# Expert rows scattered to their tokens' rows instead of gathered, and unread matmuls at the start

## The chip, the cores and the metric

The kernel runs on one core of a Trainium2 chip. A core has five engines that run side by side, each in its own order: PE (TensorE, matmuls and the weight loads before them), DVE (VectorE), ACT (ScalarE), POOL (GpSimd) and SP (SyncE, which here only issues DMAs). SP, ACT and POOL issue DMAs, which all run on the core's 16 DMA engines. Data lie in HBM (DRAM), in SBUF (128 partitions) or in PSUM (eight banks, written by PE). The metric is the device time of one launch in microseconds; lower is better.

## The reference, cut to what matters

`x` is 625 x 1024; there are 20000 edges, sorted by `dst`, each of one of two types.

```
edge_index = jnp.stack([src, dst])
x = x + gnn(layernorm(x), edge_index, edge_type_2, ...)
x = x + ffn(layernorm(x))

gnn(h):  n = t5_layer_norm(h)
         out = n @ W_root + bias
         for r in range(2):  out += segment_sum((n[src] @ W_rel[r]) * w_r, dst) / max(cnt_r, 1)
         return h + elu(out) @ wo

ffn(h):  shared = mean over 2 of (gelu(h @ sW1 + sb1) @ sW2 + sb2)
         gates  = h @ rW + rb;   top 2 of 8, softmax over the two
         moe    = sum over the two chosen experts e of  w_e * (gelu(h @ W1[e] + b1[e]) @ W2[e] + b2[e])
         return shared + moe
```

## The kernel before

`gnn_ffn_kernel` runs `sparse_kernel`, and `dense_kernel` only if a flag says that the inputs don't fit the sparse layout; with these inputs it is not run. The framework keeps each engine's instructions in the order of the program unless one isn't ready in its own planning, and it sets the waits. `tc.issue_after(ins)` puts what is issued inside it behind `ins` on the same engine.

**Front.** The edges are turned into counts per (dst, src) pair by matmuls of one-hot rows. `edge_columns` brings the edge lists into columns (four transposes, `p_edge`). `count_windows` walks over 160 chunks `c` in groups of up to four: DVE writes the one-hots `oh_s` (L845, L846) and `oh_k` (L849), PE multiplies them (L858) into PSUM. Between the chunks the list `after[c]` runs other work at fixed `c`: `stats(t)` (mean and variance of the token tile `t`, and a centred copy `h` on ACT, L758), `to_columns(t, ...)` (eight transposes into `p_t`, L786, evicted by ACT, L792, and DVE, L789, into `nT`), `scales` (square roots on ACT, L709), `project(i)` (p_pr, 8 blocks of K that each show as two matmuls, L879), later `aggregate` and so on. `stats(0)` comes before the loop, behind `edge_columns`. The list `evicted` holds the last ACT and DVE evictions of tile 0; three orders are hung on it: ACT's square roots for two tiles come after `evicted[0]`, `stats(t)` for t > 0 after `evicted[1]`, and the one-hots of c = 8 after `evicted[1]`. All inputs come over SP in the order edges, x tile 0, W_root, x tile 1, tiles 2 and 3, tile 4, W_rel, wo.

**Middle.** The node projections and aggregations give `xh`; its layernorm goes to DRAM as `h2d`, `xh` itself as `x1d` (POOL, L953 and L954). `gate`, `route` and `slots` choose the two experts of each token and give each of the 2 x 625 (token, choice) pairs a slot in one of NJ = 11 tiles of 128 slots. Four tiles (NM2, numbers 0 to 3) hold halves or quarters of several experts, seven (`whole`) one expert each. `slots` makes `tok` (which token each slot holds, by ten small matmuls `p_tok` of one-hots with the token numbers `tid`), `idx` (in which slot each token's pair lies) and the flag `over`. PE runs the shared experts' first layer meanwhile. `fetch` gathers each tile's token rows from `h2d` with an indirect DMA on POOL (L1287), `expert_in` and `expert_mid` make the hidden rows `hjT`.

**End.** For each tile in `ORDER`, PE multiplies `hjT` with the experts' second weights into `p_yj` (L1382); where a tile holds several experts, ACT has copied their weights to `w2m` (L1374). DVE or ACT copies the two halves to `y` (L1386, L1388), and SP stores `y` plainly to DRAM: the first NA = 5 tiles to `ya`, the other six to `yb` (L1390). Then 20 indirect DMAs on POOL gather the rows back in token order: ten from `ya` after the fifth tile, ten from `yb` after the last (L1363); each `g[d, a]` holds token tile `d`'s choice `a` and is filled by both, since rows out of bounds are left alone. `w2m`, `y` and `g` share a pool of 15 buffers of 512 KB. PE goes on with the shared experts' second layer, `p_o` (L1429, L1431), five token tiles in eleven pieces, and DVE adds `p_o` and the weighted `g` to `x1` in an order fixed by `added` (L1405): p_o of tile 0, g of tile 0, p_o of tile 1, g of tile 1, then all g of tiles 2 to 4, then the other p_o. `store` sends each tile's rows to the output, 112 rows from SP and 13 from ACT (L1413); the last tile goes out in three pieces. The weights `sw2` and the rows `x1` for this stage are loaded from POOL before it (L1351, L1354).

Of the kernel before, what the change touches and what calls it, by code (L numbers as in the profile page):

```python
# [8 lines left out]
F32 = mybir.dt.float32  # L9
F16 = mybir.dt.float16  # L10
# [7 lines left out]
N = 625  # L18
D = 1024
# [24 lines left out]
NH2 = 3  # L44
NM2 = NH2 + 1
NQ = NJ - NM2
NA = NM2 + 1
HS = 64
QS = 32
NM = 5  # L50
# [402 lines left out]
def sparse_kernel(  # L453
# [34 lines left out]
    h2d = dram.tile([N, D], F32, name="h2d")  # L488
    x1d = dram.tile([N, D], F32, name="x1d")

    ya = dram.tile([NA * 128, D], F32, name="ya")
    yb = dram.tile([(NJ - NA) * 128, D], F32, name="yb")

    def ps_acc(name):
        return psum.tile([128, 512], F32, tag="acc", name=name, bufs=5)
# [74 lines left out]
    for m in range(NT):  # L570
# [7 lines left out]
    it = const.tile([TP, 128], F16, name="it")  # L578
    nc.gpsimd.iota(it, pattern=[[1, 128]], base=0, channel_multiplier=0,
                   allow_small_or_imprecise_dtypes=True)  # L580
    tid = const.tile([TP, NT], F16, name="tid")
    nc.gpsimd.iota(tid, pattern=[[TP, NT]], base=0, channel_multiplier=1,
                   allow_small_or_imprecise_dtypes=True)

    nt = 2 * NH2 + NQ
# [116 lines left out]
    def rsqrt(v, eps, name, n=1):  # L702

        c = small.tile([TP, 4, NT], F32, tag="rsq", name=name)
        c = [c[:, i, :n] for i in range(4)]
        with ExitStack() as order:
            if n == 2:
                order.enter_context(tc.issue_after(evicted[0].ins))
            nc.scalar.activation(c[3], v, AF.Sqrt, bias=epsc[eps])  # L709
        nc.vector.reciprocal(c[0], c[3])  # L710
        nc.vector.scalar_tensor_tensor(c[1], v, eps, c[0], op0=ALU.add, op1=ALU.mult)
        nc.vector.scalar_tensor_tensor(c[2], c[1], -0.5, c[0], op0=ALU.mult, op1=ALU.mult)
        r = small.tile([TP, NT], F32, tag="rsqo", name=name + "o")[:, :n]
        nc.vector.scalar_tensor_tensor(r, c[2], 1.5, c[0], op0=ALU.add, op1=ALU.mult)
        return r
# [61 lines left out]
    evicted = []  # L777
    nT = fbig.tile([128, KD, N], F32, name="nT")

    def to_columns(t, row, colT, scaled):  # L780
# [41 lines left out]
    def count_windows(between):  # L822
        accs = {}
        for cs in groups:
# [141 lines left out]

    for t, (c0, c1) in enumerate(((0, 3), (4, 9), (13, 19), (16, 22), (20, 26))):
        if t:
            at(c0, stats, t)
        at(c1, to_columns, t, None, nT, True)  # L970
    at(30, transpose_vec)
    at(6, scales, 0, 2)
    at(18, scales, 2, 4)
# [127 lines left out]

    idx = const.tile([TP, 2, 2, NT], I32, name="idx")
    wab = const.tile([TP, 2, NT], F32, name="wab")
    tok = const.tile([128, NJ], I32, name="tok")
    ej = const.tile([1, nt + 4], I32, name="ej")

    def slots():
# [79 lines left out]
        nc.vector.tensor_scalar(full, full, 127, None, op0=ALU.bitwise_and)  # L1189

        pc = const.tile([TP, 2, 2, NT], F16, name="pc")
        nc.vector.tensor_copy(pc[:, 0], full)
# [4 lines left out]
        for a in range(2):  # L1197
            nc.vector.tensor_tensor(oh[:, a], it[:, None, :].to_broadcast([TP, NT, 128]),
                                    pc[:, 0, a][:, :, None].to_broadcast([TP, NT, 128]), op=ALU.is_equal)
            nc.vector.tensor_tensor(oj[:, a], it[:, None, :NJ].to_broadcast([TP, NT, NJ]),  # L1200
                                    pc[:, 1, a][:, :, None].to_broadcast([TP, NT, NJ]), op=ALU.is_equal)
            nc.vector.tensor_mul(oj[:, a], oj[:, a], tid[:, :, None].to_broadcast([TP, NT, NJ]))
# [25 lines left out]
        over = const.tile([1, 3], F32, name="over")  # L1228
        nc.vector.tensor_tensor(over[:, 0:1], end_w[:1, NE - 1 :], taken[:1, 0:1], op=ALU.add)
        nc.vector.tensor_scalar(over[:, 0:1], over[:, 0:1], NQ + NH2 + 0.5, None, op0=ALU.is_gt)  # L1230
        nc.vector.tensor_scalar(over[:, 1:2], end_h[:1, NE - 1 :], 2 * NH2 + 0.5, None, op0=ALU.is_gt)
        nc.vector.tensor_scalar(over[:, 2:3], end_q[:1, NE - 1 :], 4.5, None, op0=ALU.is_gt)
        nc.vector.tensor_reduce(flagf[:, 1:2], over, axis=AX.X, op=ALU.add)
        nc.vector.tensor_tensor(flag, flagf[:, 0:1], flagf[:, 1:2], op=ALU.add)
        return named

# [119 lines left out]
    gs = {}  # L1356

    def gather(part, src):
        for d in range(NT):
            for a in range(2):  # L1360
                if part == 0:
                    gs[d, a] = gat.tile([128, D], F32, tag="y", name=f"g_{d}_{a}")[:TP]
                nc.gpsimd.indirect_dma_start(  # L1363
                    out=gs[d, a], out_offset=None, in_=src,
                    in_offset=bass.IndirectOffsetOnAxis(ap=idx[:, part, a, d : d + 1], axis=0),
                    bounds_check=src.shape[0] - 1, oob_is_err=False)

    ORDER = (*whole[:1], *range(NM2), *whole[1:])
    w2m = {}
    for j in ORDER:  # L1370
        for a, _, e in parts(j)[1:]:
            for k in range(HK):
                w2m[j, a, k] = gat.tile([128, D], F32, tag="y", name=f"w2m_{j}_{a}_{k}")
                nc.scalar.copy(w2m[j, a, k][:, None, :], w2a[:, bass.ds(e, 1), k, :])  # L1374
    for n, j in enumerate(ORDER):
        y = gat.tile([128, D], F32, tag="y", name=f"ys_{j}")
        for s in range(2):
            at = slice(s * 512, (s + 1) * 512)
            p = ps_acc(f"p_yj_{j}_{s}")
            for k in range(HK):  # L1380
                for a, b, e in parts(j):
                    made = nc.tensor.matmul(p[a:b], hjT[:, j, k, a:b],  # L1382
                                     w2m[j, a, k][:, at] if a else w2a[:, bass.ds(e, 1), k, at],
                                     start=(k == 0), stop=(k == HK - 1))
            if s or n < NA - 1:
# [18 lines left out]

    def add_experts(d):
        for a in range(2):
            add(x1[:, d, :], gs[d, a], wab[:, a, d : d + 1], x1[:, d, :])

    def store(d, at):
        for g, eng in zip(PARTS, (nc.sync, nc.scalar)):
# [67 lines left out]
```

## Time and profile before

| What | us |
|---|---|
| Three timed runs, median (lowest to highest) | 316.52 (314.95 to 316.57) |
| The profiled execution: its own time | 315.64 |
| its span, first to last instruction | 313.8 |
| PE, first matmul of the counts | 9.56 |
| PE busy in the span | 294.8 (94%) |
| DVE busy in the span | 179.5 (57%) |
| ACT, POOL busy | 110.5, 65.3 |
| DMA issues, median to landing: `ya`, `yb` stores (512 KB) | 7.2, 5.6 |
| gathers `g` from `ya`, from `yb` | 6.7, 8.6 |
| gathers `xs` in the middle | 4.4 |

The span is the profiler's time from the first to the last instruction; the launch's own time has 1.8 us around it. A busy row of the profile has 40 digits, each the busy share in tenths of a slice of 7.8 us. A group of instructions is written as line, engine, operation, what is written from what, the shapes and the count, then busy us and mean ns of one, then the idle time of the engine ahead of them and what ended it. A wait is written as the engine and line that waited, whom it waited for, the us in total, how often, and the longest. A line of the timeline has the start, the duration and, in brackets, the idle time before it. Matmuls overlap in the pipeline, so a matmul's duration is longer than the distance between two starts; that distance is the rate.

### The profile page before, as it was taken

What the parts mean: (1) busy time and instruction counts of PE and PEld (TensorE: products, weight loads), DVE (VectorE), ACT (ScalarE), POOL (GpSimd) and SP (SyncE); (2) the same over time, 40 slices, a digit from 0 to 9 for tenths busy, and PEclk for the clock granted to TensorE, in tenths of its full rate; (3) what the DMA queues carried; (4) which work ended last, traced back from release to release, by engine and by line L of the source; (5) the groups of instructions that cost most, each with busy time, mean ns of one, the idle gap of its engine ahead of it and who ended that gap; (6) DMA issues with size and microseconds to landing.
All of it is one profiled execution on the core that took longest, in us unless ns stands there. A gap on an engine that the chain in (4) does not pass through costs nothing. (4 is left out here: it accounts for less than half of the span.)

```text
span 313.8 us, 4738 instructions
## 1 busy us (share of the span) xinstructions
PE 294.8 (94%) x1629; PEld 201.1 (64%) x1629; DVE 179.5 (57%) x538; ACT 110.5 (35%) x248; POOL 65.3 (21%) x113
## 2 busy tenths in 40 slices
PE   1799999999999999999999999999999999999980
PEld 1687777787888763557777788877745344444450
DVE  4899999977879676873893122212124121105690
ACT  3456123332437245335323235638269211000000
POOL 9500000000000012431131022110050048348300
PEclk9999999999999999999999999999999999999997
DMA  7993000000000499999999563340059946838915
GB/s 227 323 342 112 1 2 0 1 2 0 2 0 2 148 326 317 390 392 385 340 380 409 229 195 89 120 135 1 2 181 332 392 168 200 255 106 210 273 41 170
DMA packets 33048, 56.48 MB, mean 180 GB/s; under 512 B 8966, under 2 KB 22797, under 8 KB 33013
## 3 DMA queue, kind: packets, MB, share of 16 engines
q1 hardware_dynamic: 19444, 34.39, 31.4%
q0 software_dynamic: 13280, 21.37, 21.8%
q10 hardware_dynamic: 294, 0.35, 0.5%
q8 instruction: 15, 0.25, 0.3%
q14 instruction: 15, 0.11, 0.1%
HBM read 47.76 MB, written 13.57 MB: 195 GB/s over the span
## 5 line engine op out<-in xcount | busy, mean ns | idle before, releaser
L879 PE MATMUL p_pr<-wg,nT 128*125 128x286 f32 x240 | 63.4, 416 | 0.0
L879 PEld LDWEIGHTS p_pr<-wg,nT 128*125 128x125 f32 x240 | 44.7, 192 | 12.2 <-ACT nT L792 0.3
L1314 PE MATMUL p_h<-w1a,xsT 128*128 (+2 forms) x176 | 40.0, 380 | 0.0
L1382 PE MATMUL p_yj<-w2a,hjT 128*128 (+2 forms) x88 | 38.6, 594 | 0.0
L1429 PE MATMUL p_o<-sw,shT 128*125 128x512 f32 (+1 forms) x88 | 36.1, 553 | 0.0
L1096 PE MATMUL p_sh<-h2T,sw 128*128 128x313 f32 (+1 forms) x128 | 35.2, 428 | 0.0
L1314 PEld LDWEIGHTS p_h<-w1a,xsT 128*128 128x128 f32 (+2 forms) x176 | 28.7, 168 | 7.4 <-issue 0.5
L1096 PEld LDWEIGHTS p_sh<-h2T,sw 128*128 128x128 f32 x128 | 23.7, 189 | 8.6 <-issue 0.2
L1429 PEld LDWEIGHTS p_o<-sw,shT 128*125 128x125 f32 x88 | 16.4, 187 | 16.9 <-issue 16.2
L1386 DVE COPY ys<-p_yj 128x512 f32<-128x512 f32 x15 | 10.4, 691 | 29.1 <-PE p_yj L1382 29.1
L954 POOL DMA_DIRECT2D x1d<-xh x10 | 5.3, 533 | 103.4 <-DVE xh L947 103.3
L1382 PEld LDWEIGHTS p_yj<-w2a,hjT 128*128 128x128 f32 (+2 forms) x88 | 14.4, 168 | 16.5 <-issue 16.5
L1318 DVE COPY hj<-p_h 128x256 f32<-128x256 f32 x11 | 4.7, 424 | 31.1 <-PE p_h L1314 31.1
L849 DVE TENSOR_TENSOR ohk<-iotk,cols 125x512 f16<-125x512 f16 (+4 forms) x49 | 22.1, 451 | 0.0
L858 PE MATMUL cnt<-ohk,ohs 125*128 125x128 f16 x223 | 17.8, 222 | 4.3 <-DVE ohs L846 4.3
L845 DVE TENSOR_TENSOR ohs<-iota,cols 125x512 f16<-125x512 f16 (+3 forms) x49 | 18.0, 367 | 6.8 <-PE cnt L858 6.8
L1287 POOL DMA_INDIRECT xs<-h2d,tok x11 | 11.4, 1040 | 45.6 <-PE p_x L1295 33.4
L897 PE MATMUL p_agg<-P,CT 125*125 125x287 bf16 x150 | 20.4, 286 | 0.2 <-DVE P L887 0.2
L858 PEld LDWEIGHTS <-ohs 125*128 125x128 f16 x223 | 14.9, 99 | 8.6 <-DVE ohs L846 5.0
L1405 DVE SCALAR_TENSOR_TENSOR x<-g,wab,x 125x1024 f32<-125x1024 f32 x10 | 12.6, 1283 | 12.8 <-DMA g<-yb,idx 12.7
L940 PE MATMUL p_y<-wo_t,eT 128*125 128x512 f32 x40 | 19.2, 603 | 0.0
L897 PEld LDWEIGHTS <-CT 125*125 125x125 bf16 x150 | 18.4, 137 | 0.1
(292 smaller groups left out, 434.8 us busy)
## 6 DMA issues: line engine op xcount, KB each, us to landing
w1a<-in_L_ffn_W_dram SPq DMA_DIRECT2D x8, 1024.0 KB, 18.4
w2a<-in_L_ffn_W_dram SPq DMA_DIRECT2D x8, 1024.0 KB, 17.0
yb<-ys SPq DMA_DIRECT2D x6, 512.0 KB, 5.6
ya<-ys SPq DMA_DIRECT2D x5, 512.0 KB, 7.2
x<-x1d POOLq DMA_DIRECT2D x5, 500.0 KB, 13.3
wg<-in_L_gnn_W_rel_dram SPq DMA_DIRECT2D x2, 1144.0 KB, 19.1
x1d<-xh POOLq DMA_DIRECT2D x5, 448.0 KB, 6.6
h2d<-h POOLq DMA_DIRECT2D x5, 448.0 KB, 6.4
```

Source lines behind the costliest of these rows:

```text
L845: nc.vector.tensor_tensor(os, row[:, None].to_broadcast(shape), key, op=ALU.is_equal)
L849: nc.vector.tensor_tensor(halves(oh_k[:, :g, :kn]), row[:, None].to_broadcast(shape), key, op=ALU.is_equal)
L858: nc.tensor.matmul(accs[w][:, : R * WD], oh_s[:, i, :], oh_k[:, i, (w - lo) * 128 : (w - lo + 1) * 128], start=first, stop=last)
L879: nc.tensor.matmul(p[:TP, :F], nT[:, k, m * TP : (m + 1) * TP], wg[:, k, r, :], start=(k == 0), stop=(k == KD - 1))
L897: nc.tensor.matmul(p[:TP, : F + 1], CT[:, m, at : at + TP], P[:, m, r, i], start=(m == 0 and i == 0), stop=(m == NT - 1 and i == 2))
L940: nc.tensor.matmul(ps[s][:TP, :], eT[:, k, :], wo_t[:, k, s * 512 : (s + 1) * 512], start=(k == 0), stop=False)
L1096: nc.tensor.matmul(p[:, : z - a], sw1[:, i, k, t * 128 : (t + 1) * 128], h2T[:, k, a:z], start=(k == 0), stop=(k == KD - 1))
L1287: nc.gpsimd.indirect_dma_start(out=xs, out_offset=None, in_=h2d, in_offset=bass.IndirectOffsetOnAxis(ap=tok[:, j : j + 1], axis=0))
L1314: nc.tensor.matmul(p[a:b, :H], xsT[j][:, k, a:b], w1m[j, a][:, 0, k, :] if a else w1a[:, bass.ds(e, 1), k, :], start=(k == 0), stop=(k == ...
L1382: made = nc.tensor.matmul(p[a:b], hjT[:, j, k, a:b], w2m[j, a, k][:, at] if a else w2a[:, bass.ds(e, 1), k, at], start=(k == 0), stop=(k = ...
L1405: added.append(nc.vector.scalar_tensor_tensor(*args, op0=ALU.mult, op1=ALU.add))
L1429: nc.tensor.matmul(p[:TP, :n], shT[:, i, k, own], sw2[:, i, k, at], start=(i == 0 and k == 0), stop=False)
```

## The change

- At PE's start, `warm(24)` ahead of `edge_columns` and `warm(40)` behind `transpose_lnw` issue matmuls of `iota` with itself into a PSUM tile that nothing reads.
- The three orders are hung on a new list `second` (the end of `stats(1)` on DVE, and its `h` on ACT): ACT's square roots for two tiles come after the `h` of tile 1, `stats(t)` for t > 1 and the one-hots of c = 8 after `stats(1)`.
- `ya` and `yb` become one tensor `yt` of 2 x 1024 rows. At c = 50 it is filled with zeros: POOL sets a tile to zero, SP writes it out twice.
- `slots` no longer makes `idx`. The token numbers in `tid` count from 1, with 1024 added for the second choice, so that `p_tok` gives both the token of a slot (`tok`) and the row of `yt` that it belongs to (`row`); an empty slot gets a row beyond the bounds. `over` is worked out on all partitions ahead of `p_tok` and multiplies `tid`.
- `sw2` and `x1` are loaded from SP, not POOL. `ORDER` puts three whole tiles, not one, ahead of the four mixed ones.
- Each `y` is scattered to its rows of `yt` by an indirect DMA on POOL when it is made; the scatters are declared independent of one another. After the last, SP loads the ten `g` plainly, 128 rows each.

```diff
-NA = NM2 + 1
+YB = 1024
...
-    ya = dram.tile([NA * 128, D], F32, name="ya")
-    yb = dram.tile([(NJ - NA) * 128, D], F32, name="yb")
+    yt = dram.tile([2 * YB, D], F32, name="yt")
...
-    tid = const.tile([TP, NT], F16, name="tid")
-    nc.gpsimd.iota(tid, pattern=[[TP, NT]], base=0, channel_multiplier=1,
+    tid = const.tile([TP, 2, NT], F16, name="tid")
+    nc.gpsimd.iota(tid, pattern=[[YB, 2], [TP, NT]], base=1, channel_multiplier=1,
...
             if n == 2:
-                order.enter_context(tc.issue_after(evicted[0].ins))
+                order.enter_context(tc.issue_after(second[1].ins))
...
-            with tc.issue_after((evicted[1] if t else behind).ins):
+            with tc.issue_after((second[0] if t > 1 else evicted[1] if t else behind).ins):
                 nc.vector.bn_stats(st[:, s, :], xh[:TP, t, s * 512 : (s + 1) * 512])
...
-            nc.scalar.activation(h, xh[:TP, t, :], AF.Identity, bias=neg)
+            moved = nc.scalar.activation(h, xh[:TP, t, :], AF.Identity, bias=neg)
+        if t == 1:
+            second.extend((last, moved))
...
             elif c0 == 2 * GROUP:
-                order.enter_context(tc.issue_after(evicted[1].ins))
+                order.enter_context(tc.issue_after(second[0].ins))
...
+    def warm(n):
+        for _ in range(n):
+            nc.tensor.matmul(scrap[:, :128], iota, iota, start=True, stop=True)
+
+    scrap = ps_acc("scrap")
+    warm(24)
     behind = edge_columns()
     transpose_lnw()
+    warm(40)
     ahead = stats(0)
...
+    def clear():
+        nc.gpsimd.memset(zero, 0.0)
+        for a in range(2):
+            to = bass.AP(tensor=yt.tensor, offset=yt.offset + (a * YB + 1) * D, ap=[[D, 128], [128 * D, NT], [1, D]])
+            nc.sync.dma_start(to, zero[:, None, :].to_broadcast([128, NT, D]))
+
+    at(50, clear)
...
-        nc.vector.tensor_scalar(ab, ab, float(NJ * 128 - 1), None, op0=ALU.min)
-        low = const.tile([TP, 2, NT], F32, name="low")
-        nc.vector.tensor_scalar(low, ab, float(NA * 128), 4096.0, op0=ALU.is_lt, op1=ALU.mult)
-        nc.vector.scalar_tensor_tensor(idx[:, 1], ab, -float(NA * 128), low, op0=ALU.add, op1=ALU.add)
-        nc.vector.tensor_copy(idx[:, 0], ab)
...
+        over = const.tile([TP, 5], F32, name="over")
+        nc.vector.tensor_tensor(over[:, 0:1], end_w[:, NE - 1 :], taken[:, 0:1], op=ALU.add)
...
+        nc.vector.tensor_reduce(over[:, 3:4], over[:, :3], axis=AX.X, op=ALU.add)
+        nc.vector.tensor_scalar(over[:, 4:5], over[:, 3:4], 0.5, None, op0=ALU.is_lt)
+        nc.vector.tensor_scalar(tid, tid, over[:, 4:5], None, op0=ALU.mult)
...
-        named = nc.vector.tensor_scalar(tok, q[:, :NJ], float(N - 1), None, op0=ALU.min)
+        t = rt.tile([128, 2, NJ], F32, name="t")
+        nc.vector.tensor_scalar(t[:, 0], q[:, :NJ], float(YB), float(YB), op0=ALU.is_ge, op1=ALU.mult)
+        nc.vector.scalar_tensor_tensor(t[:, 1], q[:, :NJ], -1.0, t[:, 0], op0=ALU.add, op1=ALU.subtract)
+        named = nc.vector.tensor_scalar(tok, t[:, 1], 0.0, float(N - 1), op0=ALU.max, op1=ALU.min)
+        nc.vector.tensor_scalar(t[:, 0], q[:, :NJ], 0.5, 4.0 * YB, op0=ALU.is_lt, op1=ALU.mult)
+        nc.vector.tensor_tensor(row, t[:, 0], q[:, :NJ], op=ALU.add)
...
-        nc.gpsimd.dma_start(sw2[:, i], sW2[i].rearrange("(k p) d -> p k d", p=128))
+        nc.sync.dma_start(sw2[:, i], sW2[i].rearrange("(k p) d -> p k d", p=128))
...
-        nc.gpsimd.dma_start(x1[:, t, :], x1d[t * TP : (t + 1) * TP, :])
+        nc.sync.dma_start(x1[:, t, :], x1d[t * TP : (t + 1) * TP, :])
...
-    ORDER = (*whole[:1], *range(NM2), *whole[1:])
+    ORDER = (*whole[:3], *range(NM2), *whole[3:])
...
-        first = n < NA
-        nc.sync.dma_start((ya if first else yb)[(j - (0 if first else NA)) * 128 :][:128], y)
-        if n == NA - 1:
-            gather(0, ya)
-    gather(1, yb)
+
+        sent.append(nc.gpsimd.indirect_dma_start(
+            out=yt, out_offset=bass.IndirectOffsetOnAxis(ap=row[:, j : j + 1], axis=0), in_=y, in_offset=None,
+            bounds_check=2 * YB - 1, oob_is_err=False))
+        for s in sent[:-1]:
+            tc.declare_no_dep(sent[-1].ins, s.ins, reason="rows of different slots")
+
+    gs = {}
+    for d in range(NT):
+        for a in range(2):
+            at = a * YB + 1 + d * TP
+            gs[d, a] = gat.tile([128, D], F32, tag="y", name=f"g_{d}_{a}")
+            nc.sync.dma_start(gs[d, a], yt[at : at + 128, :])
```

More of the change, by code (lines that the diff above doesn't have):

```diff
@@ L775, in add_h @@
                                        op0=ALU.mult, op1=ALU.add)
-    evicted = []
+    evicted, second = [], []
     nT = fbig.tile([128, KD, N], F32, name="nT")
@@ L970, in sparse_kernel @@
         at(c1, to_columns, t, None, nT, True)
+    zero = fbig.tile([128, D], F32, name="zero")
+    def clear():
[4 more added lines that the diff above has]
+    at(50, clear)
     at(30, transpose_vec)
@@ L1098, in shared_in @@
             nc.scalar.activation(shT[:, i, t, a:z], p[:, : z - a], AF.Gelu, bias=vT[:, b : b + 1])
-    idx = const.tile([TP, 2, 2, NT], I32, name="idx")
     wab = const.tile([TP, 2, NT], F32, name="wab")
     tok = const.tile([128, NJ], I32, name="tok")
+    row = const.tile([128, NJ], I32, name="row")
     ej = const.tile([1, nt + 4], I32, name="ej")
@@ L1189, in slots @@
         nc.vector.tensor_scalar(full, full, 127, None, op0=ALU.bitwise_and)
+        over = const.tile([TP, 5], F32, name="over")
+        nc.vector.tensor_tensor(over[:, 0:1], end_w[:, NE - 1 :], taken[:, 0:1], op=ALU.add)
+        nc.vector.tensor_scalar(over[:, 0:1], over[:, 0:1], NQ + NH2 + 0.5, None, op0=ALU.is_gt)
+        nc.vector.tensor_scalar(over[:, 1:2], end_h[:, NE - 1 :], 2 * NH2 + 0.5, None, op0=ALU.is_gt)
+        nc.vector.tensor_scalar(over[:, 2:3], end_q[:, NE - 1 :], 4.5, None, op0=ALU.is_gt)
+        nc.vector.tensor_reduce(over[:, 3:4], over[:, :3], axis=AX.X, op=ALU.add)
+        nc.vector.tensor_scalar(over[:, 4:5], over[:, 3:4], 0.5, None, op0=ALU.is_lt)
+        nc.vector.tensor_scalar(tid, tid, over[:, 4:5], None, op0=ALU.mult)
         pc = const.tile([TP, 2, 2, NT], F16, name="pc")
@@ L1201, in slots @@
                                     pc[:, 1, a][:, :, None].to_broadcast([TP, NT, NJ]), op=ALU.is_equal)
-            nc.vector.tensor_mul(oj[:, a], oj[:, a], tid[:, :, None].to_broadcast([TP, NT, NJ]))
+            nc.vector.tensor_mul(oj[:, a], oj[:, a], tid[:, a, :, None].to_broadcast([TP, NT, NJ]))
         shared_in(0, 1)
@@ L1227, in slots @@
         nc.vector.tensor_scalar(ej, es[:, : nt + 4], float(NE - 1), None, op0=ALU.min)
[L1228 to L1233, printed above, removed]
+        nc.vector.tensor_copy(flagf[:, 1:2], over[:1, 3:4])
         nc.vector.tensor_tensor(flag, flagf[:, 0:1], flagf[:, 1:2], op=ALU.add)
@@ L1350, in sparse_kernel @@
     for i in range(NS):
-        nc.gpsimd.dma_start(sw2[:, i], sW2[i].rearrange("(k p) d -> p k d", p=128))
+        nc.sync.dma_start(sw2[:, i], sW2[i].rearrange("(k p) d -> p k d", p=128))
     x1 = late.tile([TP, NT, D], F32, name="x1")
     for t in range(NT):
-        nc.gpsimd.dma_start(x1[:, t, :], x1d[t * TP : (t + 1) * TP, :])
+        nc.sync.dma_start(x1[:, t, :], x1d[t * TP : (t + 1) * TP, :])
     gat = pool(ctx, "gat", 15, side="right")
[L1356 to L1366, printed above, removed]
-    ORDER = (*whole[:1], *range(NM2), *whole[1:])
+    ORDER = (*whole[:3], *range(NM2), *whole[3:])
     w2m = {}
@@ L1374, in sparse_kernel @@
                 nc.scalar.copy(w2m[j, a, k][:, None, :], w2a[:, bass.ds(e, 1), k, :])
+    sent = []
     for n, j in enumerate(ORDER):
@@ L1384, in sparse_kernel @@
                                      start=(k == 0), stop=(k == HK - 1))
-            if s or n < NA - 1:
+            if s or n < 4:
                 nc.vector.tensor_copy(y[:, at], p)
@@ L1408, in add_experts @@
         for a in range(2):
-            add(x1[:, d, :], gs[d, a], wab[:, a, d : d + 1], x1[:, d, :])
+            add(x1[:, d, :], gs[d, a][:TP], wab[:, a, d : d + 1], x1[:, d, :])
     def store(d, at):
```

## The prediction

> **What bounds the kernel now.** I read the busy rows first, then each end of the span by windows, waits and timeline.
>
> ```profile
> PE   1799999999999999999999999999999999999980
> DVE  4899999977879676873893122212124121105690
> POOL 9500000000000012431131022110050048348300
> PEclk9999999999999999999999999999999999999997
> ```
>
> Forty slices of 7.8 us. PE is full from the second slice to the last but one, so only three things can move the end: a faster PE, fewer PE waits, or what lies before its first and after its last matmul. Listing start-to-start distances by shape, I find almost no wait in between. The clock row reads 9 from the start, but the groups by form say otherwise; first 9.5 to 15.4 us, then 16 to 24 us (mean ns of one is the last figure before the bar):
>
> ```profile
> L879 PE MATMUL p_pr<-wg,nT 128*125 128x286 f32 x7 | 3.6, 697 | 0.0
> ```
>
> ```profile
> L879 PE MATMUL p_pr<-wg,nT 128*125 128x286 f32 x25 | 6.5, 410 | 0.0
> ```
>
> The same product starts every 0.48 us until the one begun at 15.50, and every 0.24 after it. PE ran at half rate from its first real work at 9.56 to about 15.7: 6.2 us, of which 3.1 are the penalty.
>
> At the other end, waits from 268 to 314 us, then the timeline:
>
> ```profile
> DVE x L1405 <- DMA g<-yb,idx: 12.7, 4, 8.1
> DVE x L1405 <- PE p_o L1431: 5.9, 2, 3.0
> ```
>
> ```profile
> 284.43 1.28 DVE L1405 SCALAR_TENSOR_TENSOR x<-g,wab,x 125x1024 f32<-125x1024 f32 x1 [8.13 <-DMA g<-yb,idx]
> ...
> 302.82 3.73 DVE L1405 SCALAR_TENSOR_TENSOR x<-p_o,x 125x512 f32<-125x512 f32 x7
> ...
> 304.55 0.27 PE L1431 MATMUL p_o<-b,wT 96*125 96x256 bf16 x1
> ```
>
> DVE waits for gathered rows, then works off a backlog: seven p_o additions in a row end at 306.55, while PE ended at 304.82. So the last 1.7 us of compute are the gather's. The stores pile up too: four of the five tiles' rows go out in a burst, the store before the last holds SP for 1.55 us (others 0.32), the last is issued at 308.22, lands at 311.6, and 2.1 us of closing waits follow.
>
> **The change, part by part.**
>
> *Unread products.* 24 matmuls of 128 columns, fp16, then 40. A cold one starts every 0.107 us (cnt rows at 9.64, 9.75, 9.86). iota is ready at 1.23, so 24 fill 1.3 to 3.9; p_edge's input is ready only at 4.0, p_lnw ends at 5.4, and 40 more last to 9.7 cold or about 7.6 warm. Real work begins at 9.56: cost 0, at most 0.1. Does the rate double in time? The row: 6.2 us from first steady work to full rate, hence about 7.5 here. The Trainium skill, "TensorE: Matmul & The Clock Gate", Part 1, says a free-running window of 3.4 us must be busy, and the half rate returns after such a window idle. Its "whatever you issue in your first ~3.4 µs runs at 1.2 GHz" would make today's penalty 1.7 us; the row says 3.1, and I take the row. The idle gap left before 9.56 is 0.6 to 2 us, which no row here tests; by the page it is short enough. Both ends: 0 and 3.1.
>
> *What PE's gain meets.* Work from 9.56 at full rate: counts, transposes (8 x 0.107), then the 16 of p_pr, led by ACT's evictions, end near 14.9 instead of 17.79, so 2.9. Then DVE, busy 29.8 of 32 us between 8 and 40. Waits from 8 to 31 us:
>
> ```profile
> DVE nT L789 <- PE p_t L786: 1.9, 2, 1.3
> ```
>
> I set each group's first counting matmul beside the end of its one-hots on DVE: the slack is 2.9, 3.4, 2.0, 0.49, 0.54, 0.72 us for the groups at c = 8, 12, 13, 17, 20, 24, then 3.8 and over 5. DVE's own gain: stats(1) started at 12.47 and can't start before x's second tile lands, 11.74 in the DMA's landing records, so 0.7; the idle 0.6 before 18.96 goes too. The edited orders put stats(1) and its ACT copy ahead of one-hots and of ACT's square root, which makes h(1) ready at 14.7 (was 15.73), when PE wants it. After those, at 13.45, DVE has what it had from 13.67 to 22.79, less 0.6 idle and 0.25 already done: 8.3 us, so c = 17's one-hots end at 21.7 (was 22.79). PE starts that group at 21.75 instead of 23.28: **1.5 us**. Groups 20 and 24 shift alike. Bounds: 2.9 if DVE's order lets PE by; below, see the memset.
>
> *Does it reach the end?* Waits from 40 to 106 us:
>
> ```profile
> DVE ohs L845 <- PE cnt L858: 6.8, 6, 2.2
> ```
>
> DVE has 6.8 us of waits for PE there, the last (1.59) at 90.97, so it takes up 1.5 before the tight groups at 98 and 102 us (slack 0.06 and 0.30). Weight loads after 104 wait for the last one-hots and move along.
>
> *Zero fill.* POOL memset of 128x1024: the nearest row, iota 128x1280, is 1.33, so 1.1 us, near 15 us, where POOL is free. The Trainium skill, "SBUF — State Buffer", section "SBUF: two separate sides", speaks against it: GpSimd and a fast-mode DVE instruction exclude one another for a whole instruction. That would take 1.1 from a DVE without slack: 1.5 becomes 0.4. The row: POOL's add at 9.16 (0.45 us) lies across DVE's one-hots, and one start slips by 0.06. I take 0. The two DMAs (2.6 MB each) follow wo_r on SP, after 19.9 us. W_rel and wo_t are ahead of them in the queue; DMA is idle from 28 to 104 and SP idle to 104.7. At 350 GB/s they are done by 40: free; without that cover, 15 us.
>
> *Slot arithmetic.* Four small DVE operations go, two join before p_tok and three `over` ones move ahead of it; rows are 0.13 to 0.17 each, 0.07 back to back. p_tok has no slack on PE (160.42), so up to 0.1 there. tok and row, four more: first fetch 0.4 later, but it landed near 166 and is used at 178.3. Free.
>
> *Queues.* sw2 and x1 loads (seven, 4.6 us of POOL) go to SP, where nothing waits behind them; they landed by 252 and are needed at 268 and 272. POOL is free for the first scatter at 233.9. Order of tiles: w2m is needed later; fifteen buffers hold twelve w2m and three y, so the fourth tile's copy can wait some 1.3 us on DVE, while PE has five banks. Free.
>
> *Scatters and loads.* 20 gathers and 11 stores go; 11 scatters and 10 loads come. No row scatters; nearest are the gathers, 0.94 to 1.26 us on POOL, 4.4 to landing when alone. Tiles come every 3.43 us, so no queue. Last y copied at 269.05; scatter lands about 274.5. Ten loads of 512 KB start then: 5.2 MB at the 332 to 392 GB/s of the slices from 235 to 251 is 14.5 us, first pair at 279, last at 291 (was 284 and 298.5). Ten additions (1.28) and the p_o ones then reach the fourth tile before 298. DVE idles for PE, and the last addition runs from 304.87 to 305.28 instead of to 306.55: 1.27. The last store goes out at once, 305.35 instead of 308.22: 2.87 in all; landing in an emptier queue may give 0.5 more. I take **3.0**; bounds 1.3 (burst remains) and 3.7. Until the first pair is 5 us later than costed, it costs nothing.
>
> **Sum.** 1.5 + 3.0 = 4.5. The profiled run took 315.64 (span 313.8 and 1.8 around it), which gives 311.1. The median of the three runs is 316.52, 0.9 above it; from it, **312.0**, which I predict.
>
> **Rivals.** (1) *Front lost*: DVE, x's landing or the memset hold PE; for it DVE's slack of half a us, against it 1.9 us of DVE's waits. Tail only: 313.5. (2) *Front whole*: a better DVE order: 2.9 + 3.0, 310.6. (3) *Tail lost*: plain loads land as late as gathers, the old stores having taken up to 8 us to land; against it, that landing ran beside gathers. Front only, 315.0. (4) *Slower*: POOL's scatter is dear. The chain is first y at 233.9, 11 scatters of c, 9 us to land and load a pair, then DVE without a pause: ten additions at 1.25, seven of p_o at 0.6, two at 0.33, 17.4 us. The last addition ends at 260.3 + 11c. Below c = 3.43 POOL keeps pace with the tiles; today's 306.55 is passed at c = 4.2. If each waited for its predecessor's landing, c = 1.3 + 4.4 = 5.7, the end is 323, and 316.5 - 1.5 + 16.5 gives 331.5. Against it: 1.26 rows, and the dependence between scatters declared away.
>
> **Numbers.** Forecast 0.60 (own range 310 to 314.5), rivals 0.15, 0.12, 0.08, 0.05. A measurement tells about 0.5% from no change, 1.6 us: faster is below 314.9. Forecast, first and second rival lie there nearly whole, the third mostly within: 0.86, 0.09, 0.05. Range 309.8 to 315.0.
>
> **What shows it.** p_pr at 0.24 from its first; no 697 ns mean. The c = 17 counts near 21.7. POOL scatters of 1.0 to 1.3 us, 3.4 apart. First g about 279; additions waiting on p_o at the end, not on g; last store issued under a us after PE's end. Wrong if PE is still cold after 9.56, if counts wait for one-hots more than costed, or if g comes after 284.

## The result

The changed kernel takes **311.21 us** (median of 4 runs, 310.76 to 312.2) against 315.79 for the kernel before in the same session: ratio 0.986, 95% interval 0.9817 to 0.9902. Forecast were 312.0 us (from 316.52, the median of the three runs known then) and a gain of 4.5; the medians show 4.6. The profiled run took 312.2 us, with a span of 310.0 (before: 315.64 and 313.8). The total came out nearly as worked out. Its two parts did not: by the medians of the runs below, the front is worth 0 to 0.5 us instead of 1.5, and the tail 3.3 to 3.9 instead of 3.0. The two errors nearly cancel, so the close total is luck.

From the page of the changed kernel: the busy rows of PE, DVE and POOL and the clock row, in tenths, then a row of the groups and one of the DMA issues:

```profile
PE   8799999999999999999999999999999999999991
...
DVE  4899999977879676873895032122214211256920
...
POOL 9600000000000012431112032120002232200000
PEclk9999999999999999999999999999999999999999
...
L1403 POOL DMA_INDIRECT yt<-ys,row x11 | 10.8, 984 | 50.5 <-DVE ys L1399 50.5
...
g<-yt SPq DMA_DIRECT2D x10, 512.0 KB, 7.7
```

PE is now busy in the first slice (the unread products), and DVE's last slice but one fell from 9 to 2, because it no longer works off a backlog. A scatter holds POOL for 0.98 us and then waits for the next tile. The first product of the projection, groups by form from 10.8 to 14.8 us:

```profile
L880 PE MATMUL p_pr<-wg,nT 128*125 128x286 f32 x16 | 4.1, 410 | 0.0
```

The mean of 410 ns is what the kernel before reached only after 16 us; sixteen of them start between 10.84 and 14.55. What comes next, in the waits from 8 to 31 us (us in total, times, longest):

```profile
PE cnt L859 <- DVE ohs L847: 2.7, 3, 1.9
...
DVE st L749 <- DMA xh<-in_x_dram: 1.1, 1, 1.1
```

So DVE is the bound as forecast (1.9 of the 2.7 us lie ahead of the first counts, at 9.49), and it stood 1.1 us for x's second tile, which landed at 12.53 in this execution (11.74 before). The end, waits from 268 to 314 us and then the timeline from 300:

```profile
DVE x L1426 <- PE p_o L1452: 16.3, 7, 3.0
...
DVE x L1426 <- DMA g<-yt: 0.4, 1, 0.4
```

```profile
303.28 0.27 PE L1452 MATMUL p_o<-b,wT 96*125 96x256 bf16 x1
303.59 0.42 DVE L1426 SCALAR_TENSOR_TENSOR x<-p_o,x 125x256 f32<-125x256 f32 x1 [1.42 <-PE p_o L1452]
```

DVE's waits for gathered rows, 12.7 us before, are 0.4; its last addition waits 1.42 us for PE. The last store is issued at 304.04 (before 308.22).

Between the two profiled spans lie 3.8 us, which add up as follows: PE's last matmul starts 1.27 us sooner (303.28 for 304.55), the last store is issued 2.91 us sooner than that explains, and it lands 0.37 us later after its issue (3.78 for 3.41).

### The profile page after: what moved, and what is told of

It is laid out like the page before. It is cut to its first block, busy times and chain, and to the rows that moved or that the text cites. A ratio compares the mean times of both kernels' runs of the same rounds, so it can differ in the third digit from the quotient of the medians.

```text
span 310.0 us, 4844 instructions
## 1 busy us (share of the span) xinstructions
PE 297.6 (96%) x1693; PEld 200.9 (65%) x1693; DVE 180.7 (58%) x541; ACT 110.1 (36%) x248; POOL 46.7 (15%) x98
## 4 chain that ended last, share of the span: by engine, by line
PE 78%; DVE 14%; DMA 3%; ACT 1%; issue 1%; SPq 1%; ACTq 0%
PE p_h L1337 12%; PE p_yj L1395 12%; PE p_pr L880 11%; PE p_o L1450 11%; PE p_sh L1115 10%; PE p_y L941 5%; PE p_agg L898 4%; DMA xh<-in_x_dram 3%; PE p_x L1318 3%; DVE ohk L850 2%; PE p_t L787 2%; DVE ohs L847 2%; DVE ohs L846 2%; PE cnt L859 2%; PE p_y L945 1%; DVE ct L808 1%
## 5 line engine op out<-in xcount | busy, mean ns | idle before, releaser
L880 PE MATMUL p_pr<-wg,nT 128*125 128x286 f32 x240 | 61.9, 408 | 0.0
L880 PEld LDWEIGHTS p_pr<-wg,nT 128*125 128x125 f32 x240 | 43.4, 187 | 11.9 <-ACT nT L793 0.4
L1403 POOL DMA_INDIRECT yt<-ys,row x11 | 10.8, 984 | 50.5 <-DVE ys L1399 50.5
L847 DVE TENSOR_TENSOR ohs<-ohs,cols 125x512 f16<-125x512 f16 (+3 forms) x49 | 18.1, 369 | 0.0
```

The costliest lines, as they stand in the source:

```text
L847: nc.vector.tensor_tensor(os, os, both(VV_, 128)[1], op=ALU.mult)
L880: nc.tensor.matmul(p[:TP, :F], nT[:, k, m * TP : (m + 1) * TP], wg[:, k, r, :], start=(k == 0), stop=(k == KD - 1))
L1403: sent.append(nc.gpsimd.indirect_dma_start(out=yt, out_offset=bass.IndirectOffsetOnAxis(ap=row[:, j : j + 1], axis=0), in_=y, in_offset=No ...
```

## The experiments

Twelve different kernels ran, two of them twice. Each time one execution was profiled, which gave the dates below (us). "Full rate" is when the distance between PE's matmuls halves for good; "x tile" is the landing of x's second tile; "PE" the start of the last matmul; "store" the time from there to SP's last store; "landing" from its issue to the last of its landing records. The median time is over all executions.

| kernel | full rate | x tile | PE | store | landing | span | median time |
|---|---|---|---|---|---|---|---|
| before | 15.86 | 11.74 | 304.55 | 3.67 | 3.41 | 313.8 | 315.58 |
| e8, before again | 13.01 | 11.73 | 303.57 | 3.47 | 3.81 | 313.0 | 315.47 |
| e2, products only | 4.95 | 12.15 | 303.31 | 4.57 | 2.99 | 313.0 | 315.65 |
| e4, front only | 8.69 | 12.44 | 303.68 | 3.93 | 3.49 | 313.2 | 315.05 |
| e10, tail, old tile order | 15.94 | 12.05 | 304.44 | 0.77 | 2.59 | 309.9 | 312.18 |
| e5, tail only | 14.12 | 11.84 | 303.26 | 0.77 | 3.03 | 309.2 | 311.37 |
| e1, no products | 14.91 | 12.01 | 303.86 | 0.77 | 2.44 | 309.2 | 311.13 |
| changed | 5.19 | 12.53 | 303.28 | 0.77 | 3.78 | 310.0 | 311.21 |
| a2, changed again | 14.70 | 12.78 | 303.59 | 0.77 | 2.83 | 309.3 | 311.36 |
| e7, six fills | 9.41 | 11.94 | 303.02 | 0.77 | 2.82 | 309.2 | 310.98 |
| e9, late loads | 9.00 | 12.22 | 302.97 | 0.77 | 2.67 | 308.2 | 310.59 |
| e3, old orders | 10.13 | 12.08 | 302.72 | 0.77 | 3.84 | 309.4 | 310.88 |
| e6, x sooner | 10.54 | 9.23 | 302.48 | 0.77 | 2.61 | 307.9 | 310.18 |
| e11, x sooner, no products | 13.40 | 9.48 | 303.03 | 0.77 | 2.87 | 308.7 | 311.31 |

The experiments ran in three groups, each on its own chip: e1 to e4, then a2 and e5 to e7, then e8 to e11. The kernel before ran beside each, with medians of 315.58, 315.31 and 315.22; ratios are to these. Three columns vary with nothing in the kernel: the landing, between 2.44 and 3.84 us for one and the same last store; the full rate; and x's tile, between 11.73 and 12.78 where it is loaded second. So a single profile tells the parts to some tenths of a us only where these are read off.

### Front and tail apart: e1 to e4

**e1**: the changed kernel without the products.

```diff
-    scrap = ps_acc("scrap")
-    warm(24)
...
-    warm(40)
```

> The changed kernel without its 64 unread products; orders, scatter and plain loads stay. Theory (the products are worth what the traces show of the front, about 1.0 us at PE's end, since DVE limits the rest of the 3 us): p_pr starts 0.48 us apart until near 15.5, the c = 17 counts near 23.2, time about 312.2 (the changed kernel, 311.2, plus 1.0). Rival A (PE's rate is worth the whole 3 us): about 314.2. Rival B (the three edited orders make the front's gain, not the products): 311.2 to 311.5.

Measured: 311.13 us (310.99 to 311.95), ratio to before 0.9854 (0.9818 to 0.9891). PE ran at half rate until 14.91, and the kernel is no slower than the changed one. That is the time of rival B; its cause, the edited orders, falls with e3 and e5, which have the old orders and lose nothing.

**e2**: the kernel before with the products alone.

```diff
+    scrap = ps_acc("scrap")
+    warm(24)
     behind = edge_columns()
     transpose_lnw()
+    warm(40)
```

> The kernel before with the 64 unread products added and nothing else; 20 gathers and old orders stay. Theory (the tight group at c = 17 had 0.49 us of slack on DVE, so with the old orders PE can gain no more than about that before DVE holds it): PE at full rate from the first p_pr, PE's end 0.4 to 0.6 us earlier, time 315.3. Rival A (products alone bring the front's 1.0): 314.8. Rival C (products bring nothing without the orders, or the last of the gathers eats it): 315.8.

Measured: 315.65 us, ratio 0.9999 (0.998 to 1.0019): rival C. In the profile PE ended 1.24 us sooner than in the first profile of before (0.26 sooner than in e8, the second), and the median shows none of it. From the timeline of e2 from 300 us:

```profile
299.55 2.60 DVE L1412 SCALAR_TENSOR_TENSOR x<-g,wab,x 125x1024 f32<-125x1024 f32 x2
...
302.07 3.74 DVE L1412 SCALAR_TENSOR_TENSOR x<-p_o,x 125x512 f32<-125x512 f32 x7
303.31 0.27 PE L1438 MATMUL p_o<-b,wT 96*125 96x256 bf16 x1
303.38 4.88 SPq L1420 DMA_DIRECT2D out_dram<-x  x5
```

PE is done at 303.6, but DVE still adds gathered rows until 302.1 and then has seven backlogged p_o additions to do. The stores of the last three tiles, five issues on SP, go out in one burst. From PE's last start to the last issue it is 4.57 us instead of 3.67. Of the 1.24 us, 0.75 reached DVE's backlog (302.07 for 302.82) and 0.35 the last issue: the first gather from `yb` started 1.37 us sooner than before (276.57 for 277.94), but the last landed no sooner (298.66 for 298.54). With the old tail the gathers set the end, not PE. In e8, the kernel before once more, PE was 0.98 us sooner and the last issue 1.18 (307.04 for 308.22), so how much of PE's gain passes differs from one execution to the next.

**e3**: the changed kernel with its three orders hung on the first tile's eviction again.

```diff
-                order.enter_context(tc.issue_after(second[1].ins))
+                order.enter_context(tc.issue_after(evicted[0].ins))
...
-            with tc.issue_after((second[0] if t > 1 else evicted[1] if t else behind).ins):
+            with tc.issue_after((evicted[1] if t else behind).ins):
...
-                order.enter_context(tc.issue_after(second[0].ins))
+                order.enter_context(tc.issue_after(evicted[1].ins))
```

> The changed kernel with its three edited orders hung on the first tile's eviction again, as before; products, scatter and loads stay. Theory: h(1) is late on ACT again (near 15.5), PE loses about 0.5 us of the 1.0 it won, time 311.7. Rival B (the orders are worth the front's whole gain): 312.2. Rival D (the orders are worth nothing, x tile 1's landing decides): 311.2.

Measured: 310.88 us (310.3 to 311.79), ratio 0.9841 (0.9804 to 0.9878): no slower, as rival D had it, and PE ended 0.56 us sooner than in the changed kernel. From the waits of e3 from 8 to 31 us:

```profile
PE p_t L787 <- ACT h L757: 0.5, 2, 0.3
...
DVE st L749 <- DMA xh<-in_x_dram: 0.3, 1, 0.3
PEld L859 <- DVE ohs L847: 0.2, 1, 0.2
```

The premise of the theory fell: with PE at full rate the old orders release stats(1) at 12.10, and h(1) starts on ACT at 14.22, about the changed kernel's 14.30. The one-hots of c = 8 need not wait for stats(1) any more and are ready at 14.52 instead of 15.27. PE's wait for them, 0.54 us after 14.55 in the changed kernel, is gone; it waits 0.21 for h(1) instead, and 0.17 instead of 0.56 for the one-hots of c = 13. Some of it is x's tile, 0.45 us sooner in this execution; so the edited orders bring nothing, and may cost some tenths of a us.

**e4**: products and the three orders put into the kernel before (the diffs of e2 and of e3 turned round), with stores, gathers and tile order of before.

> The kernel before with the products and the three edited orders, but with stores, 20 gathers and the old order of tiles: the front of the change without its tail. Theory: PE ends 1.0 us sooner, and gathers and backlog move along: 314.8, so that the tail is worth the remaining 3.6 to the changed kernel's 311.2. Rival E (the gathers' landing, not PE, sets the end, so that a faster front meets the same gathers): 315.5 to 315.8, and front and tail are not additive.

Measured: 315.05 us, ratio 0.9984 (0.9966 to 1.0003). PE ended 0.87 us sooner than in the first profile of before; of that 0.6 reached the last store's issue. The time lies between theory (314.8) and rival E (315.5), and its interval (314.5 to 315.7) holds both. Rival E's mechanism is in the trace: a third of PE's gain is lost to the gathers.

### Is it the tail alone? a2 and e5

**a2** is the changed kernel once more, unedited.

> The changed kernel once more, unedited, beside the next three. In the first four runs PE's earlier end did not show in the time (0.6 us at PE between the changed kernel and the one without products, and no difference in the medians). Theory F (the front's gain passes to the end, but a straggling last store hides it in single runs): 310.6 to 311.2, and shorter than e5_tail_only by about 1. Theory T (nearly all of the 4.5 us is the tail's): as e5_tail_only within 0.4.

**e5** takes out the products (e1's diff) and the three orders (e3's), so that in the front the order of PE's and DVE's instructions is that of before.

> The changed kernel without its products and with the orders of before: the tail (scatter, plain loads, order of tiles, zero fill) alone; PE's and DVE's order in the front is that of before, row for row. Theory F (front and tail add): PE ends 0.3 us before the kernel before (order of tiles alone), time 312.1, the tail worth 3.5. Theory T: 311.2, the tail worth 4.4. The forecast on record had 313.5 for this.

Measured: 311.36 us (310.48 to 312.41) and 311.37 us (310.98 to 311.91); ratios to before 0.9869 (0.9837 to 0.9901) and 0.9873 (0.9844 to 0.9902). Theory T, in the times: the tail alone gives the changed kernel's. Six runs of each leave some 0.8 us either way (an estimate from their spread), so a front worth 1.5 would have shown, one worth 0.5 would not. The two profiles say how it went in these two executions. Groups by form from 11.3 to 16 us, first of a2, then of e5:

```profile
L880 PE MATMUL p_pr<-wg,nT 128*125 128x286 f32 x13 | 4.9, 549 | 0.3 <-DMA wg<-in_L_gnn_W_root_dram 0.3
```

```profile
L880 PE MATMUL p_pr<-wg,nT 128*125 128x286 f32 x12 | 4.1, 500 | 0.0
```

A mean between 410 (full) and 697 (half) is a mixture. In a2 the products did their work: PE was at full rate by 4.87. It stood idle from 7.12 to 9.62, ran its counts at full rate until 10.88, waited for W_root, which landed at 11.24 in this execution (9.45 in the changed kernel's first profile), and from 11.98 to 14.70 it was at half rate again. In e5, without products, full rate came at 14.12, where the kernel before had needed until 15.86. Even where the products held, in the changed kernel's first profile, PE's last matmul starts no sooner than e5's (303.28 and 303.26), though x's tile landed 0.69 us later there.

### Is the full rate a draw? e8

**e8** is the kernel before once more, unedited.

> The kernel before once more, unedited, for a second profile. Theory (when PE reaches full rate is a draw that differs from execution to execution: 15.86 in the first profile, 14.12 and 14.91 in two kernels with no products): full rate somewhere from 13.5 to 16.5, PE's end moved by half the difference, 303.9 to 304.9, and what lies behind PE as before (last store issued 3.4 to 3.9 us after PE's last start, landing 3.0 to 3.5 after that). Rival (the date belongs to the kernel): full rate at 15.8 to 15.9 again, PE's end at 304.5.

Its groups by form from 11.3 to 16 us:

```profile
L879 PE MATMUL p_pr<-wg,nT 128*125 128x286 f32 x15 | 4.3, 440 | 0.0
```

Measured: full rate from 13.01, 2.85 us sooner than in the first profile of the same kernel, and PE's end 0.98 us sooner (303.57). So the date is a draw, as the theory had it: chance sets it anew in each execution. It fell even outside the range expected (13.5 to 16.5, with PE's end at 303.9 to 304.9), and the landing, 3.81, lies above its 3.0 to 3.5. The half rate's length belongs to the execution: without products, from the first steady matmul near 9.6 to full rate, it was 6.3, 3.5, 6.3, 4.5, 4.9 and 3.9 us (before, e8, e10, e5, e1, e11). Only the late dates cost: e8 (13.01) and e5 (14.12) end together once the 0.3 us of the tile order (e10) is set off, and the two near 15.9 end 1 us later.

### The tile order: e10

**e10** is e5 with the old order of result tiles.

```diff
-    ORDER = (*whole[:3], *range(NM2), *whole[3:])
+    ORDER = (*whole[:1], *range(NM2), *whole[1:])
```

> The changed kernel without products, with the orders of before and with the order of result tiles of before: scatter, plain loads and zero fill alone. Theory (the 0.3 us between the first p_yj and the first p_o, 38.8 us before and 38.5 after, is the order of tiles): 38.8 us again, time 0.3 more than e5_tail_only: 311.7. Rival (the gathers' traffic cost PE the 0.3): 38.5 us, time 311.4. Full rate of PE is a draw here too, between 13.5 and 16.5.

Measured: 312.18 us (312.01 to 312.48), ratio 0.9902 (0.9867 to 0.9937). First p_yj to first p_o is 38.78 us, with the new order 38.48 in all nine profiles that have it: the 0.3 is the tile order's, as the theory had it. The time is 0.8 over e5's instead of 0.3. In the profiles a later full rate adds 0.9 at PE; what it was in the other runs isn't seen. e10 drew nearly the full-rate date of before (15.94 and 15.86), so the two profiles show the tail alone: last store 2.90 us sooner behind PE, landing 0.8 sooner, span 313.8 to 309.9. Which part of the tail's change brings this (scatter, plain loads, SP in place of POOL) was not taken apart.

### The costs put at nothing: e7 and e9

**e7** fills `zero` six times over.

```diff
-        nc.gpsimd.memset(zero, 0.0)
+        for _ in range(6):
+            nc.gpsimd.memset(zero, 0.0)
```

> The changed kernel with the fill of zero done six times over on POOL (the same zeros; all rows of PE and DVE keep their order), so that POOL writes for some 6.3 us beside DVE's tightest stretch. Theory (POOL's fill does not hold DVE, as the single one of 1.05 us beside one-hots of 0.42 showed): the one-hots keep 0.42 and 0.22, groups c = 13 to 20 start as in the changed kernel, time 311.2. Rival (POOL's fill and DVE's fast form exclude one another): DVE loses up to 5 us between 15 and 21, the c = 20 counts come up to 5 us later, and after DVE's waits for PE have taken up what they can, time 312 to 315.

Measured: 310.98 us (310.83 to 312.37), ratio 0.9866 (0.9836 to 0.9897). The timeline of e7 from 15.6 us, then one line of the changed kernel's:

```profile
15.69 4.00 POOL L985 MEMSET zero<- 128x1024 f32 x4
...
16.07 0.41 DVE L847 TENSOR_TENSOR ohs<-ohs,cols 125x512 f16<-125x512 f16 x1
...
17.73 0.96 DVE L766 COPY rstd<-ln_0o 125x2 f32<-125x2 f32 x1
17.80 0.90 DVE L749 BATCH_NORM_STATS2 st<-xh 125x6 f32<-125x512 f32 x1
```

```profile
18.32 0.16 DVE L766 COPY rstd<-ln_0o 125x2 f32<-125x2 f32 x1
```

The one-hots keep their 0.42 us beside the fills. The copy of two columns, 0.16 us in the changed kernel, takes 0.96. One of the fills begins at 17.72, just ahead of the copy, and ends at 18.67, as the copy does. The statistics behind it take 0.90 us instead of 0.68, and DVE loses 0.33 us in all (from their start to the next instruction's it is 0.93, in the changed kernel 0.60). That is the exclusion that the forecast weighed ("SBUF — State Buffer", section "SBUF: two separate sides" of the Trainium skill). As this section has it, a copy can be shut out by a fill, but an instruction with two inputs only by a GpSimd one that reads SBUF, and a fill only writes; the two cases here agree. In the changed kernel the single fill is over at 15.85, ahead of the copy at 18.32. In e3 and e6 the old orders put the copy inside it, at 15.45 and 15.21, and there it takes 0.58 and 0.57 us; the next one-hots keep their length.

**e9** puts four unread loads ahead of the ten of g.

```diff
+    for i in range(4):
+        spare = gat.tile([128, D], F32, tag="y", name=f"spare_{i}")
+        nc.sync.dma_start(spare, yt[1 + i * 128 : 129 + i * 128, :])
```

> The changed kernel with four more loads of result rows, into tiles that nothing reads, ahead of the ten on the same queue: 2.1 MB, 5 to 6 us at the 360 GB/s of those slices. Theory (the loads have some 5 us of slack, as the forecast said): first pair of g lands near 281 (275 to 277 without), last near 295, DVE works it off before the last tile's products, the end moves by less than 0.4 us, time 311.0 to 311.7. Rival (g's landing sets the end): 3 to 6 us more, 314 to 317.

Measured: 310.59 us (310.15 to 311.75), ratio 0.9859 (0.9818 to 0.99), a little below the range of the theory and far from the rival. From DVE's rows of its timeline from 268 us:

```profile
274.03 0.69 DVE L1429 SCALAR_TENSOR_TENSOR x<-p_o,x 125x512 f32<-125x512 f32 x1 [2.91 <-PE p_o L1455]
...
280.89 2.60 DVE L1429 SCALAR_TENSOR_TENSOR x<-g,wab,x 125x1024 f32<-125x1024 f32 x2 [6.17 <-DMA g<-yt]
...
283.41 1.28 DVE L1429 SCALAR_TENSOR_TENSOR x<-p_o,x 125x512 f32<-125x512 f32 x2
...
284.73 10.16 DVE L1429 SCALAR_TENSOR_TENSOR x<-g,wab,x 125x1024 f32<-125x1024 f32 x8
```

g's first tile landed at 280.78 instead of 275.32, DVE waited 6.17 us for it, worked without a pause to 294.9, and the last addition ended 0.74 us after PE's last start, as in every kernel with the new tail. So loads that land 5.46 us later cost nothing.

### A version that beats both: e6 and e11

**e6** has the old orders (e3's diff) and loads x's second tile between the halves of W_root.

```diff
-    load_w(R, W_root)
-    load_x(1, 1)
+    for h in range(2):
+        nc.sync.dma_start(wg[:, 4 * h : 4 * h + 4, R, :],
+                          W_root[h * 512 : (h + 1) * 512].rearrange("(k p) f -> p k f", p=128))
+        if h == 0:
+            load_x(1, 1)
```

> The changed kernel with the old orders (PE ended 0.56 us sooner with them in e3), and W_root loaded in two halves with x's second tile between them. Theory (DVE's wait of 1.05 us for that tile at 11.5 is what holds the front): the tile lands near 11, stats(1) starts by 11.2, PE ends 0.5 to 1.0 us before e3's 303.03 (its last matmul began at 302.72), time 310.2 to 310.7. Rival (the first product then waits for W_root's second half, at 12.3, and gives it back): PE's end as e3's or later, 310.9 to 311.5.

Measured: **310.18 us** (309.71 to 310.44), ratio to before 0.9833 (0.9805 to 0.9861); a2, beside it on the chip, had 310.48 at its best. The tile landed at 9.23 (near 11 was expected), and DVE's wait for it is gone. But stats(1) began only at 11.87, not by 11.2, since it stands behind the first tile's eviction, and the products ran at half rate until 10.54. PE's end is 0.24 us before e3's, less than the 0.5 expected. The medians of e3 and e6 lie 0.7 apart; 0.3 of that is between the chips, by the kernel before beside them (315.58 and 315.31), and the rest no profile explains.

**e11** is e6 without the products.

> e6 (x's second tile between the halves of W_root, old orders) without the 64 products: does PE's rate matter once the tile is there in time? Theory (with the tile early DVE no longer holds PE, so the cold products cost their time): PE at half rate to 14 to 16, PE's end 0.8 to 1.5 us behind e6's 302.48, time 311.0 to 311.6. Rival (PE's rate is worth nothing, as between a2 and e5): 310.2, as e6.

Measured: 311.31 us (310.91 to 311.79), ratio 0.9876 (0.984 to 0.9913), 1.1 more than e6, and the ranges don't overlap. PE ended 0.55 us later, with an early draw (13.40). So here the products do pay. That x's early tile is the reason isn't shown: e3 and e5 are the same pair with the tile in its old place, and there too PE ends 0.54 us sooner with the products (302.72 and 303.26), while the medians lie 0.5 apart with overlapping ranges. The old orders, which e3 and e6 share, may be as much of it.

## Why the prediction was right in sum and wrong in its parts

**Full rate, 6.2 us of half rate and 3.1 of penalty: the step that failed.** The forecast weighed its one row against the page ("TensorE: Matmul & The Clock Gate", Part 1) and took the row as the kernel's. It was one draw, and equal to the longest seen: six executions without products took 3.5 to 6.3 us. The page's window fits all six: if it runs free and one whole window of 3.4 us must be busy, full rate comes between one window and two after the work begins, 3.4 to 6.8 us (an estimate from that page; the ±500 ns that it gives for the spread is too narrow for these runs). Read so, page and row agreed, and the penalty was about 2.4 on average (half of the mean, 4.9), of which DVE's work hides a part. e8 had by luck (0.98 us at PE's end) what the front was to bring.

**Full rate "about 7.5" with the products.** It was 4.87 to 5.19 at the latest in three executions (the changed kernel, a2, e2) and 8.7 to 10.5 in five (e4, e9, e7, e3, e6), always before the first p_pr. In a2 and e2 the distance halves already among the edge columns' transposes, at 4.4 and 4.6, which is 3.1 and 3.3 us after the first product: a little under one window, so the estimate does not cover them.

**The idle gap, called harmless.** 2.1 us of it cost nothing in the changed kernel and in e2. In a2 2.5 us of it, 1.3 us of counts at full rate and the break for W_root were followed by 2.7 us of half rate. The page's bound for losing the rate, an idle window of 3.4 us, was not reached there; which of the breaks did it stays open.

**What PE's gain meets.** The mechanism was right: p_pr's sixteen start at 14.55 or before instead of 17.55, then DVE decides. Groups c = 8 and 13 had slacks of 2.9 and 2.0 us before and 0.06 after. c = 17 began at 22.00, forecast 21.75: 1.28 won instead of 1.5. The missing quarter fits x's tile, costed at 11.74 from one execution and landed at 12.53 in this one. Later small waits (0.14 to 0.23 each at 28.18, 29.13 and 63.32, in an order of work that differs from that of before) leave 0.97 at the last matmul without the tile order, and only 0.5 when the five profiles with the change's front (the changed kernel, a2, e4, e7, e9) are set against the four with the front of before (before, e8, e10, e5): means of 303.25 and 303.73, with 0.3 taken off those with the old tile order. The two sets overlap. In the times, a2 and e5 show none of it.

**The edited orders** were costed as a gain, h(1) at 14.7 for 15.73. e3 had it at 14.22 without them: a PE at full rate releases the old orders early enough.

**Zero fill, slot arithmetic, queues**: free, as costed. The forecast judged the fill by an add on POOL beside one-hots; it did not look for the copies that a fill does hold (e7, e3, e6), which cost nothing in the changed kernel. The fill's two DMAs were issued at 19.98 and 20.59 us and filled slices four and five (401 and 406 GB/s), where PE's small waits are for DVE and ACT.

**Order of tiles**, costed as free: 0.3 us faster.

**Scatters and loads.** Scatters of 0.98 us (1.0 to 1.3 forecast), the last landed at 271.7 (274.5), g's first tile at 275.32 (first pair 279), the last at 289.5 (291): sooner throughout, and in slack. Rival 4's scatter of over 4.2 us is far off.

**Tail, 3.0.** The burst was read too large: in the kernel before, the stores of the first two of the five tiles were issued at 288.66 and 294.17, and three tiles went out at the end, not four. The terms that were worked out hold all the same: 1.27 for the backlog (measured 2.00 to 0.74 behind PE, 1.26) and 2.87 for store and backlog together (2.90 from before to e10). Too small were the landing, "may give 0.5 more" and taken at about 0.1 (0.4 to 1.0 sooner in eight of ten profiles, 0.4 later in the changed kernel and e3), and the tile order's 0.3. Against them stands some 0.4 us between the last landing and the end of the run that no step had (last section). Paired by their draw, the profiled runs of before and e10 give 315.64 to 312.17, 3.5 us, and with the tile order 3.8. By medians it is 3.0 to e10, 3.3 with the tile order, and 3.9 to e5 (whose interval is 3.1 to 4.9).

**The sum** thus came out by luck: the front was taken 1.0 to 1.5 too high and the tail 0.3 to 0.9 too low. Rival 1, "front lost", was nearest to what happened, but its 313.5 left the tail too small.

## What to carry to other kernels

Where the first steady matmuls run at half rate, take a second profile of the same kernel before costing that rate, since the length of the stretch and the landing of an early load differ by microseconds from one execution to the next. A gain on PE counts only as far as PE sets the end: with gathers still landing late, 1.24 us won at PE in e2's profile moved the last store by 0.35. Cheap work ahead of the first matmul can pay (e6 against e11, 1.1 us) and can come to nothing (a2 against e5), so it is tried together with the loads and orders that the next step waits for.

## What the runs showed of the hardware

- With products from 1.28 us on, full rate came after 3.1 to 3.9 us in three executions and after 7.4 to 9.3 in five. In all of them PE's work had short breaks while the edge columns were transposed (3.7 to 5 us); whether these breaks make the difference wasn't tried.
- One scatter of 128 rows of 4 KB: 0.98 us of POOL, and 3.2 us from issue to landing with little else in flight (268.47 to 271.69); the gathers `xs` of the kernel before took 4.4.
- From the last landing record to the end of the run it is 3.9 to 4.0 us in all four profiles with the old tail, and 4.3 to 4.5 in nine of the ten with the new one (4.1 in e9). Run less span alone misleads: it is 1.8 to 1.9 with the old tail, 2.2 to 2.4 with the new one and 1.8 in e7, but in e7 the span itself goes on for 2.58 us after the landing instead of 2.13, so the sum is 4.37 as in the others. What sets it stays open.
